# Statistics by channel tiles, a late bias and later last products in a fused attention block

## The chip, the cores and the metric

The kernel runs on one core of a Trainium2 chip. The metric is the device time of one execution in microseconds (us). The time before is 2275.32 us, the median of three runs (2275.29 to 2275.84). A core has a matrix engine (TensorE, PE in the profile), a vector engine (VectorE, DVE), an activation engine (ScalarE, ACT), a general engine (GpSimd, POOL), and queues that start transfers (DMA); SyncE (SP) issues most of these here. The engines run side by side and wait for each other by semaphores. PSUM is the memory that TensorE writes its products to, SBUF the memory for everything else.

## The reference

x has 384 channels of 192 x 192 pixels. Layer 0 normalises x by groups of 12 channels, makes q, k and v by a 1 x 1 product, takes the maximum of each 2 x 2 block, applies a 3 x 3 filter per channel, and mixes channels within 8 heads by four top-k softmaxes of the q-k products over all pixels. Layer 1 normalises again, takes signs, shifts rows and multiplies by signs of weights. Cut to what matters:

```python
def _gn(v, G=32, eps=1e-5):
    B_, C_, H_, W_ = v.shape
    g = v.reshape(B_, G, C_ // G, H_, W_)
    m = jnp.mean(g, axis=(2, 3, 4), keepdims=True)
    s = jnp.var(g, axis=(2, 3, 4), keepdims=True)
    return ((g - m) / jnp.sqrt(s + eps)).reshape(v.shape)

def _L0_conv_ref(x, w_qkv, b_qkv, w_dw, b_dw, w_proj, b_proj, temperature, a1, a2, a3, a4):
    # ...
    qkv = jnp.einsum('bchw,oc->bohw', x, w_qkv) + b_qkv[None, :, None, None]
    qkv = qkv.reshape(b, 3 * c, hs, DS, ws, DS).max(axis=(3, 5))
    qkv = lax.conv_general_dilated(qkv, w_dw, (1, 1), 'SAME', feature_group_count=3 * c, ...)
    q, k, v = jnp.split(qkv + b_dw[None, :, None, None], 3, axis=1)
    # ... reshaped to (b, HEADS, C, hw), q and k divided by their norms
    attn = jnp.einsum('bhcn,bhdn->bhcd', q, k) * temperature[None]
    out = _topk_softmax(attn, C // 2) @ v * a1 + _topk_softmax(attn, C * 2 // 3) @ v * a2 \
        + _topk_softmax(attn, C * 3 // 4) @ v * a3 + _topk_softmax(attn, C * 4 // 5) @ v * a4
    out = jax.nn.gelu(out.reshape(b, c, hs, ws), approximate=False)
    out = jnp.repeat(jnp.repeat(out, DS, axis=2), DS, axis=3)
    return jnp.einsum('bchw,oc->bohw', out, w_proj) + b_proj[None, :, None, None]

x = x + _L0_conv_ref(_gn(x), ...)
x = x + _L1_conv_ref(_gn(x), ...)   # signs, a shift of rows, a product with signs of weights
```

## The kernel before

x is cut into 24 units of 8 rows (2304 KB each; 128 partitions x 3 channel tiles x 1536 pixels). The pool `big` has 8 buffers of that size. The program goes through x three times: once for the statistics, once for q, k and then v, once for the end. A scheduler orders the instructions of each engine by priority (mostly the order of the program) unless the program pins them.

In the first pass, whole units go in turn to ScalarE (every third) and VectorE:

```python
        stats = [p1.tile([P, CT, BATCH * (UPX // 512) * 6], F32, name=f"stats{i}") for i in range(NB)]
        mv = p1.tile([P, CT, NB, 2], F32, name="mv")
        acc = p1.tile([P, CT, 2, NU // SHARE], F32, name="acc")
        wg = p1.tile([NG, 3 * C], F32, name="wg")
        seen = 0
        for i in range(NU):
        for i in range(NU):
            u = NU - 1 - i
            xt = unit(u, parts=CT if u in (0, NU - 1) else 1)
            # ... cut: the last six units are kept; small, indT and wq are loaded at i == 0
            if i % SHARE == 0:
                for t in range(CT):
                    for k, f in enumerate((AF.Identity, AF.Square)):
                        junk = p1.tile([P, UPX], BF16, name="junk")
                        nc.scalar.activation(
                            junk, xt[:, t], f, accum_out=acc[:, t, k, i // SHARE : i // SHARE + 1]
                        )
            else:
                b, k = divmod(seen, BATCH)
                seen += 1
                for t in range(CT):
                    for j in range(UPX // 512):
                        at = (k * (UPX // 512) + j) * 6
                        nc.vector.bn_stats(stats[b][:, t, at : at + 6], xt[:, t, j * 512 : (j + 1) * 512])
                    if k == BATCH - 1:
                        nc.vector.bn_aggr(mv[:, t, b, :], stats[b][:, t, :])
            # ... cut: at u == NU // 2, wg = sums of the weights by group
        sums = p1.tile([P, CT, 2], F32, name="sums")
        more = p1.tile([P, CT, 2], F32, name="more")
        nc.vector.tensor_reduce(more, acc, AX.X, ALU.add)
        sq = p1.tile([P, CT, NB], F32, name="sq0")
        nc.vector.tensor_mul(sq, mv[:, :, :, 0], mv[:, :, :, 0])
        nc.vector.tensor_add(sq, sq, mv[:, :, :, 1])
        nc.vector.tensor_reduce(sums[:, :, 0], mv[:, :, :, 0], AX.X, ALU.add)
        nc.vector.tensor_reduce(sums[:, :, 1], sq, AX.X, ALU.add)
        nc.vector.scalar_tensor_tensor(sums, more, 1.0 / (BATCH * UPX), sums, ALU.mult, ALU.add)
        ps = psp.tile([NG, 2], F32, name="gsps")
        group_sums(ps, sums)

        gs = p1.tile([NG, 2], F32, name="gs")
        nc.vector.tensor_scalar_mul(gs, ps, BATCH / (NU * GRP))
        gv = p1.tile([NG, 2], F32, name="gv")
        nc.vector.tensor_scalar_mul(gv[:, 0:1], gs[:, 0:1], -1.0)
        var = p1.tile([NG, 1], F32, name="var")
        nc.vector.scalar_tensor_tensor(var, gs[:, 0:1], gv[:, 0:1], gs[:, 1:2], ALU.mult, ALU.add)
        nc.vector.tensor_scalar_add(var, var, 1e-5)
        inv_sqrt(p1, gv[:, 1:2], var, 1, "s0", NG)
        ps = psp.tile([P, CT, 2], F32, name="spread")
        spread(ps, gv)
        nc.vector.tensor_copy(rstd0, ps[:, :, 1])

        for c0, c1 in ((0, P), (P, 2 * C), (2 * C, 3 * C)):
            for t in range(CT):
                nc.vector.tensor_scalar_mul(wq[:, t, c0:c1], wq[:, t, c0:c1], rstd0[:, t : t + 1])
        nc.vector.tensor_copy(nmean0, ps[:, :, 0])
        shift = p1.tile([NG, 1], F32, name="shift")
        nc.vector.tensor_mul(shift, gv[:, 0:1], gv[:, 1:2])
        ps = psp.tile([P, NM], F32, name="bqps")
        for m in range(NM):
            nc.tensor.matmul(ps[:, m : m + 1], wg[:, m * P : (m + 1) * P], shift, start=True, stop=True)
        nc.vector.tensor_add(bq, bq, ps)
```

Then a unit's tile m (0 to 2 are q, 3 to 5 k, 6 to 8 v) is made in three blocks of three products, each reduced from PSUM by VectorE, followed by a bias on ScalarE and nine taps of the filter (the first on ScalarE, eight on VectorE):

```python
    def qkv_unit(pqkv, xt, u, m, pl, parts):


        x4 = xt.rearrange("p t (r w) -> p t r w", w=W)
        lo, hi = rows(u)
        for r0, nr, c0, ncol in BLOCKS:
            ps = pqkv.tile([P, 512], F32, name="qkv")
            for t in range(CT):
                nc.tensor.matmul(
                    ps,
                    wq[:, t, m * P : (m + 1) * P],
                    x4[:, t, r0 : r0 + nr, c0 : c0 + ncol],
                    start=(t == 0),
                    stop=(t == CT - 1),
                )
            nc.vector.tensor_reduce(
                pl[:, 2 + r0 // 2 : 2 + (r0 + nr) // 2, 1 + c0 // 2 : 1 + (c0 + ncol) // 2],
                ps.rearrange("p (i a j b) -> p i j a b", a=2, b=2, j=ncol // 2),
                AX.XY,
                ALU.max,
            )
        new = pl[:, 2 : 2 + PR, 1 : 1 + WP]
        nc.scalar.activation(new, new, AF.Identity, bias=bq[:, m : m + 1])
        for acc, r0, n in parts:
            acc2 = acc.rearrange("p (r w) -> p r w", w=WP)
            for k in range(9):
                r = lo - 1 + r0 + k // 3
                src = pl[:, r : r + n, k % 3 : k % 3 + WP]
                if k == 0:
                    nc.scalar.activation(acc2, src, AF.Identity, bias=bdw[:, m : m + 1], scale=wdw[:, m, 0:1])
                else:
                    nc.vector.scalar_tensor_tensor(acc2, src, wdw[:, m, k : k + 1], acc2, ALU.mult, ALU.add)
            # ... cut: ScalarE keeps two rows for the next unit
    pqkv = products_of_x.enter_context(tc.tile_pool(name="qkv", bufs=3, space=PSUM))
```

q and k are transposed in blocks by VectorE, moved by 32 transfers into `room`, and multiplied into `gram` one unit later; the last unit's products come in `gathered`, at the start of v:

```python
        size = -(-(PR + 1) * WP // P) * C
        blocks = wp.tile([P, 2, size], F32, name="blocks")
        nc.gpsimd.memset(blocks, 0.0)
        pool = padded(wp, 2 * CT)
        room = big.tile([P, CT, UPX], F32, name="room", tag="big").rearrange("p t n -> p (t n)")
        qkT = room[:, : 2 * size].rearrange("p (s n) -> p s n", s=2)
        # ... cut
        def products(u):

            n, nk, q, k = of_unit(u)
            for i in range(nk):
                L = min(P, n * WP - i * P)
                for t in range(CT):
                    nc.tensor.matmul(
                        gram[t][:, : BN[t] * B],
                        q[:L, t, i],
                        k[:L, B0[t] : B0[t] + BN[t], i],
                        start=u == 0 and i == 0,
                        stop=u == NU - 1 and i == nk - 1,
                    )
        # ... cut
            for m in range(2 * CT):
                acc = tp.tile([P, (PR + 1) * WP], F32, name="dw")[:, : n * WP]
                qkv_unit(pqkv, xt, u, m, pool[m], [(acc, 0, n)])
                transposed(u, *divmod(m, CT), acc)
                sq = tp.tile([P, (PR + 1) * WP], BF16, name="sq", bufs=1)
                nc.scalar.activation(sq[:, : n * WP], acc, AF.Square, accum_out=ssq[:, m, u : u + 1])
                if u and m == CT - 1:
                    products(u - 1)
                if m % CT == CT - 1:
                    moved(u, m // CT)

    def gathered():

        products(NU - 1)
        for t in range(CT):
            at = D0[t] - B0[t] * B
            nc.vector.tensor_copy(gsb[:, t, : DN[t]], gram[t][:, at : at + DN[t]])
        last_products.close()
```

In v's loop, the softmax is a generator that is advanced once for each tile from the second unit on, and the attention products follow when it is done:

```python
        wl = wp.tile([P, CT, C], F32, name="wl")
        nc.scalar.dma_start(wl, a["w_projG"].rearrange("(t p) o -> p t o", p=P))
        nc.vector.tensor_reduce(wg1, wl.rearrange("p t (g c) -> p t g c", c=GRP), AX.X, ALU.add)
        wl = wp.tile([P, CT, C], F32, name="wl")
        nc.scalar.dma_start(wl, a["weightT"].rearrange("(t p) o -> p t o", p=P))
        nc.scalar.activation(wb, wl, AF.Sign, saturate=False)
        done, steps = 0, None
        # ... cut
        for u in range(NU):
            # ... cut: the unit's load, chunk (the output of v), parts
            for m in range(CT):
                # ... cut
                qkv_unit(pqkv, xt, u, 2 * CT + m, pool[m], parts)
                if u == 0 and m == 1:
                    gathered()
                    po = vs.enter_context(tc.tile_pool(name="p4o", bufs=NP, space=PSUM))
                    psp = vs.enter_context(tc.tile_pool(name="p3ps", bufs=1, space=PSUM))
                    bg = psp.tile([P, P], F32, name="p3ps")[:NG, :1]
                    group_sums(bg, bpr.unsqueeze(2))
                    nc.vector.tensor_scalar_mul(bg1, bg, -1.0 / GRP)
                if u >= TOPK and steps is None:
                    steps = softmaxes(p3, psp)
                if steps:
                    if next(steps, 1):
                        steps = ()
                        scratch.close()
                        early = opened("p5x0", 1)
                elif steps == () and done < NAB - HOLD and (done + 1) * ABLK <= first * WP:
                    attention(done)
                    done += 1
```

## Time and profile before

| | |
|---|---|
| time, median of three runs | 2275.32 us |
| span of the profiled execution | 2274.4 us |
| PE busy | 2093.8 us (92%) |
| DVE busy | 1902.4 us (84%) |
| ACT busy | 819.4 us (36%) |
| products of q, k and v (L321) | 1683.9 us in 3888 entries, 594 ns mean |
| filter taps on DVE (L344) | 709.1 us (q and k), 370.2 us (v) |
| reductions from PSUM (L328) | 442.6 us in 648, 684 ns mean |
| statistics on DVE (L248) | 87.2 us in 144, 675 ns mean |
| statistics on ACT (L239) | 71.1 us in 48, 1482 ns mean |

A product of 32-bit numbers shows as two entries on PE (x18 for 9 products). Entries overlap with the next, so a mean duration is longer than the time from one start to the next; where the pace matters, starts are compared. In the profile, an idle time stands in brackets with what ended it, and a name such as `room<-blocks` is a transfer or an operation from the right tile to the left one. L and a number is a line of the kernel.

The stages, by the profile's time: loads and statistics to about 152 us, a chain of small operations to 161 us, q and k to about 1345 us, v to about 1970 us, the end to 2274 us.

### The profile page before, as it was taken

What the parts mean: (1) busy time and instruction counts of PE and PEld (TensorE: products, weight loads), DVE (VectorE), ACT (ScalarE), POOL (GpSimd) and SP (SyncE); (2) the same over time, 40 slices, a digit from 0 to 9 for tenths busy, and PEclk for the clock granted to TensorE, in tenths of its full rate; (3) what the DMA queues carried; (4) which work ended last, traced back from release to release, by engine and by line L of the source; (5) the groups of instructions that cost most, each with busy time, mean ns of one, the idle gap of its engine ahead of it and who ended that gap; (6) DMA issues with size and microseconds to landing.
All of it is one profiled execution on the core that took longest, in us unless ns stands there. A gap on an engine that the chain in (4) does not pass through costs nothing.

```text
span 2274.4 us, 19469 instructions
## 1 busy us (share of the span) xinstructions
PE 2093.8 (92%) x6135; PEld 995.7 (44%) x6135; DVE 1902.4 (84%) x3269; ACT 819.4 (36%) x1418; POOL 211.3 (9%) x338
## 2 busy tenths in 40 slices
PE   1029999999999999999999979999999999999998
PEld 0014444444444444444444434443444444455554
DVE  4667888888888888888888878987787888889998
ACT  4532222222222222222222212225333233397885
POOL 0000000000000000000000000000000000087775
PEclk7559999999999999999999989999999999999999
DMA  9962222232222232222222212105221212279997
GB/s 397 417 267 59 67 63 69 67 101 69 70 63 68 68 90 80 71 63 66 70 79 89 71 40 94 42 0 208 84 83 42 93 74 84 83 282 392 425 425 307
DMA packets 208727, 300.30 MB, mean 132 GB/s; under 512 B 162000, under 2 KB 164848, under 8 KB 208624
## 3 DMA queue, kind: packets, MB, share of 16 engines
q1 hardware_dynamic: 197936, 243.46, 30.8%
q10 hardware_dynamic: 10688, 55.61, 6.0%
q8 instruction: 48, 0.79, 0.1%
q14 instruction: 55, 0.45, 0.1%
HBM read 213.68 MB, written 56.62 MB: 119 GB/s over the span
## 4 chain that ended last, share of the span: by engine, by line
PE 79%; DVE 11%; DMA 6%; ACT 2%; issue 1%; SPq 1%; ACTq 0%; POOL 0%; POOLq 0%; DVEq 0%
PE qkv L321 64%; PE l1ps L743 6%; DMA xt<-in_x_dram 5%; PE yps L559 5%; DVE chunk L344 5%; PE gram L412 3%; DVE pooled L328 2%; PE ops L594 2%; DVE dw L344 1%; DVE stats L248 1%; ACT signs L724 1%; ACT chunk L342 0%; ACT pooled L335 0%; SPq L401 0%; DVE xt L751 0%
## 5 line engine op out<-in xcount | busy, mean ns | idle before, releaser
L321 PE MATMUL qkv<-xt,wq 128*128 128x512 f32 x3888 | 1683.9, 594 | 0.3 <-DVE small L294 0.3
L321 PEld LDWEIGHTS qkv<-xt,wq 128*128 128x128 f32 x3888 | 738.3, 191 | 920.3 <-issue 824.2
L344 DVE SCALAR_TENSOR_TENSOR dw<-pooled,small,dw 128x384 f32<-128x384 f32 (+2 forms) x1152 | 709.1, 616 | 118.8 <-ACT dw L342 93.7
L328 DVE TENSOR_REDUCE pooled<-qkv 128x128 f32<-128x512 f32 x648 | 442.6, 684 | 73.5 <-PE qkv L321 73.0
L344 DVE SCALAR_TENSOR_TENSOR chunk<-pooled,small,chunk 128x384 f32<-128x384 f32 (+3 forms) x696 | 370.2, 546 | 74.7 <-ACT chunk L342 57.3
L346 ACT COPY pooled<-pooled 128x196 f32<-128x196 f32 x207 | 73.6, 356 | 764.4 <-DVE dw L344 543.0
L335 ACT ACTIVATE pooled<-pooled,small 128x384 f32<-128x384 f32 x216 | 133.0, 616 | 409.4 <-DVE pooled L328 401.9
L724 ACT ACTIVATE signs<-xt,nmean 64x1536 fp8e4<-64x1536 f32 x144 | 226.5, 1573 | 49.0 <-PE yps L559 23.6
L743 PE MATMUL l1ps<-signs,wb 128*128 128x384 fp8e4 x864 | 154.5, 329 | 6.3 <-POOL signs L716 4.8
L751 DVE SCALAR_TENSOR_TENSOR xt<-l1ps,small,xt 128x768 f32<-128x768 f32 x144 | 138.9, 1009 | 6.3 <-ACT signs L724 3.6
L559 PE MATMUL yps<-chunk,wpr 128*128 128x384 f32 x396 | 138.3, 487 | 0.4 <-DVE xt L568 0.4
L568 DVE SCALAR_TENSOR_TENSOR xt<-yps,small,xt 128x768 f32<-128x768 f32 x132 | 128.0, 1012 | 12.2 <-DMA xt<-in_x_dram 4.7
L248 DVE BATCH_NORM_STATS2 stats<-xt 128x6 f32<-128x512 f32 x144 | 87.2, 675 | 60.4 <-DMA xt<-in_x_dram 60.4
L743 PEld LDWEIGHTS <-wb 128*128 128x128 fp8e4 x864 | 84.1, 97 | 80.4 <-issue 20.9
L198 PE MATMUL gsps<-sums,small 128*32 128x2 f32 x6 | 0.5, 196 | 128.2 <-DVE sums L269 128.2
L433 ACT ACTIVATE sq<-dw 128x384 bf16<-128x384 f32 (+2 forms) x144 | 75.3, 523 | 117.0 <-DVE dw L344 117.0
L302 POOL MEMSET pooled<- 128x196 f32 x9 | 2.4, 265 | 1173.2 <-DVE dw L344 1155.8
L342 ACT ACTIVATE dw<-pooled,small 128x384 f32<-128x384 f32 (+2 forms) x144 | 100.4, 698 | 2.3
L559 PEld LDWEIGHTS yps<-chunk,wpr 128*128 128x128 f32 x396 | 73.3, 190 | 41.4 <-PE yps L559 1.6
L239 ACT ACTIVATE junk<-xt 128x1536 bf16<-128x1536 f32 x48 | 71.1, 1482 | 52.1 <-DMA xt<-in_x_dram 50.9
L383 DVE STREAM_TRANSPOSE blocks<-dw 128x384 f32<-128x384 f32 (+1 forms) x144 | 82.0, 570 | 3.4
L412 PE MATMUL gram<-room 128*128 128x160 f32 (+3 forms) x438 | 68.1, 310 | 15.5 <-DMA room<-blocks 15.5
(117 smaller groups left out, 639.6 us busy)
## 6 DMA issues: line engine op xcount, KB each, us to landing
xt<-in_x_dram SPq DMA_DIRECT2D x83, 2304.0 KB, 14.0
out_dram<-xt ACTq DMA_DIRECT2D x19, 2304.0 KB, 15.4
room<-blocks SPq DMA_DIRECT2D x736, 36.0 KB, 2.0
xt<-in_x_dram SPq DMA_DIRECT2D x18, 768.0 KB, 8.9
out_dram<-xt ACTq DMA_DIRECT2D x9, 768.0 KB, 7.9
out_dram<-xt SPq DMA_DIRECT2D x6, 768.0 KB, 6.6
wq<-in_w_qkvT_dram ACTq DMA_DIRECT2D x1, 1728.0 KB, 15.7
room<-blocks SPq DMA_DIRECT2D x32, 48.0 KB, 2.1
```

The source lines that it names most:

```text
L248: nc.vector.bn_stats(stats[b][:, t, at : at + 6], xt[:, t, j * 512 : (j + 1) * 512])
L321: nc.tensor.matmul(ps, wq[:, t, m * P : (m + 1) * P], x4[:, t, r0 : r0 + nr, c0 : c0 + ncol], start=(t == 0), stop=(t == CT - 1),)
L328: nc.vector.tensor_reduce(pl[:, 2 + r0 // 2 : 2 + (r0 + nr) // 2, 1 + c0 // 2 : 1 + (c0 + ncol) // 2], ps.rearrange("p (i a j b) -> p i j ...
L335: nc.scalar.activation(new, new, AF.Identity, bias=bq[:, m : m + 1])
L342: nc.scalar.activation(acc2, src, AF.Identity, bias=bdw[:, m : m + 1], scale=wdw[:, m, 0:1])
L344: nc.vector.scalar_tensor_tensor(acc2, src, wdw[:, m, k : k + 1], acc2, ALU.mult, ALU.add)
L412: nc.tensor.matmul(gram[t][:, : BN[t] * B], q[:L, t, i], k[:L, B0[t] : B0[t] + BN[t], i], start=u == 0 and i == 0, stop=u == NU - 1 and i ...
L559: nc.tensor.matmul(ps, wpr[:, t, m * P : (m + 1) * P], o[:, t, :], start=(t == 0), stop=(t == CT - 1),)
L568: nc.vector.scalar_tensor_tensor(x5[:, m, r], yb, bpr[:, m : m + 1], x5[:, m, r], ALU.add, ALU.add)
L724: nc.scalar.activation(rows_of(sg, p, SAT[t] - HSHIFT[t][h]), xt[p, t, :].rearrange("p (r w) -> p r w", w=W), AF.Sign, bias=nmean1[p, t : ...
L743: nc.tensor.matmul(ps[:, j, : 2 * W], wb[:, t, m * P : (m + 1) * P], rows_of(sg, slice(0, P), SAT[t])[:, r0 + 2 * j : r0 + 2 * j + 2], sta ...
L751: nc.vector.scalar_tensor_tensor(blk, ps[:, :, : 2 * W], bl1[:, m : m + 1], blk, ALU.add, ALU.add)
```

## The change

It has five parts. (1) Statistics: of every unit, one channel tile goes to ScalarE and two to VectorE, with results in one tile `part` that both write; scale factors are folded into ScalarE's operations and the eps into a constant column. The scratch for it lies in `room`, which is now allocated ahead of the first pass, and the last two units arrive in three parts. (2) The zeros of `blocks` and of the padded tiles of q and k are written ahead of the first pass. (3) The bias from the group means is computed inside the first tile of q, after its products, instead of before it. (4) The last products of q and k and what follows are pinned to program order behind v's third tile instead of its second. (5) Softmax operations are pinned in program order, and the loads of w_projG and weightT with their reduction and sign move from the start of v to its units 4 and 5. The aim is less time in which TensorE stands: at the start, and where q and k pass over to v.

The diff, cut (statements that only move with the part around them are left out):

```diff
+    wg = aT.rearrange("p t c -> p (t c)")[:NG]
+    shift = ap.tile([NG, 1], F32, name="shift")
@@ ahead of the first pass
+    pairs = ctx.enter_context(ExitStack())
+    wp = right("p2w", stack=pairs)
+    size = -(-(PR + 1) * WP // P) * C
+    blocks = wp.tile([P, 2, size], F32, name="blocks")
+    nc.gpsimd.memset(blocks, 0.0)
+    padded_qk = padded(wp, 2 * CT)
+    room = big.tile([P, CT, UPX], F32, name="room", tag="big").rearrange("p t n -> p (t n)")
@@ the first pass
+        size1 = CT * BATCH * (UPX // 512) * 6
+        stats = [room[:, i * size1 : (i + 1) * size1].rearrange("p (t n) -> p t n", t=CT) for i in range(NB)]
+        junk = room[:, NB * size1 : NB * size1 + UPX // 2].bitcast(BF16)
+        part = p1.tile([P, CT, 2, NB + NU // SHARE + 1], F32, name="part")
+        measure = 1.0 / (BATCH * UPX)
+        nc.vector.memset(part[:, :, 0, NB + NU // SHARE :], 0.0)
+        nc.vector.memset(part[:, :, 1, NB + NU // SHARE :], 1e-5 * NU / BATCH)
-            xt = unit(u, parts=CT if u in (0, NU - 1) else 1)
+            xt = unit(u, parts=CT if u in (0, 1, NU - 1) else 1)
-            if i % SHARE == 0:
-                # all three tiles on ScalarE
-            else:
-                # all three tiles on VectorE
+            for t in range(CT):
+                if t == u % SHARE:
+                    at = NB + i // SHARE
+                    for k, f, scale in ((0, AF.Identity, measure), (1, AF.Square, measure**0.5)):
+                        nc.scalar.activation(junk, xt[:, t], f, scale=scale, accum_out=part[:, t, k, at : at + 1])
+                    continue
+                b, k = divmod(seen[t], BATCH)
+                seen[t] += 1
+                for j in range(UPX // 512):
+                    at = (k * (UPX // 512) + j) * 6
+                    nc.vector.bn_stats(stats[b][:, t, at : at + 6], xt[:, t, j * 512 : (j + 1) * 512])
+                if k == BATCH - 1:
+                    nc.vector.bn_aggr(part[:, t, :, b], stats[b][:, t, :])
@@ the chain after it
-        nc.vector.tensor_reduce(more, acc, AX.X, ALU.add)
-        # ... two reductions and a scaled sum more
-        nc.vector.tensor_scalar_mul(gv[:, 0:1], gs[:, 0:1], -1.0)
-        nc.vector.tensor_scalar_add(var, var, 1e-5)
-        ps = psp.tile([P, NM], F32, name="bqps")
-        for m in range(NM):
-            nc.tensor.matmul(ps[:, m : m + 1], wg[:, m * P : (m + 1) * P], shift, start=True, stop=True)
-        nc.vector.tensor_add(bq, bq, ps)
+        nc.vector.tensor_mul(sq, part[:, :, 0, :NB], part[:, :, 0, :NB])
+        nc.vector.tensor_add(part[:, :, 1, :NB], part[:, :, 1, :NB], sq)
+        nc.vector.tensor_reduce(sums, part, AX.X, ALU.add)
+        nc.vector.tensor_scalar_mul(gv[:, 0:1], ps[:, 0:1], -BATCH / (NU * GRP))
+    def bias(ps):
+        for m in range(NM):
+            nc.tensor.matmul(ps[:, m : m + 1], wg[:, m * P : (m + 1) * P], shift, start=True, stop=True)
+        nc.vector.tensor_add(bq, bq, ps)
@@ qkv_unit, after the three blocks
+        if before:
+            before(pqkv.tile([P, 512], F32, name="qkv")[:, :NM])
@@ products
-                    nc.tensor.matmul(
+                    ins = nc.tensor.matmul(
+                    if u == NU - 1:
+                        tc.keep_in_program_order(ins)
@@ q and k
-                qkv_unit(pqkv, xt, u, m, pool[m], [(acc, 0, n)])
+                qkv_unit(pqkv, xt, u, m, padded_qk[m], [(acc, 0, n)], None if u or m else bias)
@@ softmax
-        nc.vector.tensor_reduce(ss, ssq, AX.X, ALU.add)
+        tc.keep_in_program_order(nc.vector.tensor_reduce(ss, ssq, AX.X, ALU.add))
-                    nc.vector.memset(some, TAKEN)
+                    tc.keep_in_program_order(nc.vector.memset(some, TAKEN))
@@ v
-        # wl <- w_projG and its reduction to wg1, wl <- weightT and its sign to wb, ahead of v's loop
+        def weights(name):
+            wl = wp.tile([P, CT, C], F32, name="wl")
+            tc.keep_in_program_order(nc.scalar.dma_start(wl, a[name].rearrange("(t p) o -> p t o", p=P)))
+            return wl
+                if m == 0 and u == UC:
+                    wl = weights("w_projG").rearrange("p t (g c) -> p t g c", c=GRP)
+                    tc.keep_in_program_order(nc.vector.tensor_reduce(wg1, wl, AX.X, ALU.add))
+                if m == 0 and u == UC + 1:
+                    tc.keep_in_program_order(nc.scalar.activation(wb, weights("weightT"), AF.Sign, saturate=False))
-                if u == 0 and m == 1:
+                if u == 0 and m == CT - 1:
                     gathered()
```

## The prediction

> **What bounds the kernel now.** I read the windows table first: it says which engine limits each stage. Columns: window and length in us, then busy us (instructions) of PE, PEld, DVE, ACT and POOL, PE clock, DMA share, GB/s.
>
> ```profile
> 61.00:101.00 40.00, 0.00 (x0) 0.00 (x0) 28.33 (x48) 19.28 (x25) 0.00 (x0) 0.50 1.02 418
> 140.00:152.00 12.00, 0.00 (x0) 0.00 (x0) 11.89 (x22) 5.34 (x7) 0.00 (x0) 0.50 0.85 351
> 152.00:161.00 9.00, 5.84 (x31) 5.67 (x31) 5.71 (x28) 0.20 (x1) 0.22 (x1) 0.50 0.00 0
> 235.00:1267.00 1032.00, 1032.00 (x2665) 488.96 (x2664) 900.11 (x1520) 273.71 (x634) 0.00 (x0) 1.00 0.26 73
> 1340.00:1377.00 37.00, 21.46 (x67) 11.44 (x66) 21.57 (x48) 5.62 (x12) 1.54 (x6) 0.77 0.19 54
> 1377.00:1450.00 73.00, 73.00 (x176) 32.67 (x175) 67.00 (x199) 16.74 (x29) 0.00 (x0) 1.00 0.26 97
> 1450.00:1485.00 35.00, 35.00 (x82) 15.42 (x82) 34.96 (x101) 7.76 (x15) 0.00 (x0) 1.00 0.00 1
> 1552.00:1970.00 418.00, 417.93 (x1243) 178.72 (x1243) 331.02 (x614) 144.60 (x335) 2.20 (x2) 1.00 0.23 86
> ```
>
> Until 140 us the load of x is the limit (DMA share 1.0, 418 GB/s). From 161 us to about 1970 TensorE is, except in two places: 140 to 161 us, where statistics and their tail run alone, and 1340 to 1377, where PE is busy 21 of 37 us. From there to 1485 VectorE has almost no slack beside a full PE. The chain of waits names DVE lines there, but PE does not stop, so PE's own record decides.
>
> The chain of waits at the first place (start, length):
>
> ```profile
> 140.11 7.81 DVE stats L248 x13
> ...
> 155.38 1.44 PE spread L203 x6
> 156.82 3.85 PE bqps L293 x18
> ...
> 160.91 19.51 PE qkv L321 x38
> ```
>
> DVE works off two whole units (18 statistics, 0.60 us apart) after the last load it waits for; then a chain of small steps, then 18 bias entries on PE before the first product. The timelines of PE, DVE and ACT at the second place, with the idle time before an entry in brackets:
>
> ```profile
> 1344.47 0.35 PE L198 MATMUL p3ps<-small 128*32 128x1 f32 x6
> 1360.37 0.87 PE L412 MATMUL gram<-room 128*128 128x160 f32 x2 [15.54 <-DMA room<-blocks]
> 1361.03 9.83 PE L321 MATMUL qkv<-xt,wq 128*128 128x512 f32 x18
> 1393.59 135.78 PE L321 MATMUL qkv<-xt,wq 128*128 128x512 f32 x316
> ```
>
> ```profile
> 1347.15 1.85 DVE L328 TENSOR_REDUCE pooled<-qkv 128x128 f32<-128x512 f32 x3
> 1360.35 0.30 DVE L455 TENSOR_REDUCE ss<-ssq 128x6 f32<-128x144 f32 x1 [11.35 <-DMA room<-blocks]
> ```
>
> ```profile
> 1364.20 0.38 ACTq L582 DMA_DIRECT2D wl<-in_weightT_dram  x1
> 1368.06 1.16 ACT L583 ACTIVATE wb<-wl 128x1152 fp8e4<-128x1152 f32 x1 [3.02 <-DMA wl<-in_weightT_dram]
> ```
>
> PE stands 15.5 us because the first of the last q and k products comes right after v's first tile, and its operand is still being moved. The row with 316 entries runs at 135.78/316 = 0.430 us each, the same as in q and k: v is at PE's rate. A tile of v (18 entries) is 7.73 us.
>
> **What the skill says.** (1) The Trainium skill, TensorE: Matmul & The Clock Gate, "What's actually happening": the array runs at half clock after an idle window of about 3.4 us and needs about as long of work to recover. The trace agrees: after the stall 18 entries take 9.83 us instead of 7.73, and the first product phase starts with 26 entries in 14.36 us instead of 11.2. (2) The Trainium skill, DMA: Bandwidth & Descriptors, "Where 436 GB/s comes from": the port ceiling is 435 GB/s. The trace shows 418, so I expect nothing from the load. (3) The Trainium skill, Perfetto Trace Analysis, "Identifying the Most-Contended Engine": matmul busy time is a poor measure of the roofline, VectorE's a fair one. So I take PE's pace, not its 92%, and 34.96 of 35 us on DVE at its word.
>
> **The change, part by part.**
>
> *Statistics by channel tile.* Before, a unit was all DVE (9 x 0.60 = 5.44 us) or all ACT (6 x 1.61 = 9.7 us). Now each gives two tiles to DVE (3.6 us) and one to ACT (3.2 us), both under the 5.65 us between landings (DVE starts on loads at 106.2, 123.2, 128.8, 140.1). Nothing queues. Unit 1 lands by 140.1, so unit 0's last third lands at about 145.75 (estimate: one spacing later). Unit 0's first tile is ACT's; DVE's last three statistics and one aggregate (0.4) end at 148.0 instead of 152.07: 4.05 us saved. One buffer less for x (room is taken early) still leaves about six loads in flight.
>
> *Shorter chain.* From the last aggregate, five overlapped steps (0.82 us) become three (about 0.65); the eps step (0.18) and one dependency (0.08) go: 0.4 us.
>
> *Late bias.* Before, the first product started 4.09 us after the spread ended, behind the bias. Now it waits only for a copy and the first scaled weights, about 0.55 us (the scaling began 0.19 us after the copy): 3.55 us earlier. The 18 bias entries move behind tile 0's 18 products. Those last about 11 us, so PE is at full clock and they cost half of 3.85, about 1.95 us (estimate). Net 1.6 us.
>
> *Zeros ahead.* The blocks memset (2.66 us from 160.78) and the pads ended at 165.6, before the first reduction at 166.44. With products starting near 153 they would be late; moved, they cost nothing.
>
> Start of the kernel: 4.05 + 0.4 + 1.6 = about 6.0 us. Q and k then run at PE's pace, and the order of instructions there is the same.
>
> *Last products behind v's third tile.* PE removes 15.54 us of idle time, 0.35 us of the small product (now at the start), and the cold clock: from 1360.37 to 1374.07, 13.70 us for 18 product entries (7.73) and 24 gram entries (3.48 at 0.145), so 2.5 us. Against that, tile two of v needs a PSUM buffer of tile one. There are three, and DVE gets to the first reduction only at 1347.15 (0.6 us): PE waits about 3.2 us, just short of an idle window. After that DVE, which stood 11.35 us, does tile one's taps while PE does tiles two and three (15.5 us, to about 1363, on the old clock); the moved operand is there at 1360.3. No other wait. Net 15.54 + 0.35 + 2.5 - 3.2 = 15.2 us.
>
> *Softmax and weights later.* The softmax steps (about 20.5 us of DVE in start-to-start spacing, another 1.26 for the reduction of w_projG) now all fall from v's fourth tile on, two or three us of them that used to sit in the stall. I walked through the changed DVE order with these costs: reduction 0.60, tap 0.53 if another operation stands between, 0.655 if not, small operations at their spacing. From tile 6 to tile 18 DVE needs about 94 us against PE's 93, having fallen about 2.5 us behind at the first softmax step. PE can run 5.2 us ahead (two blocks of 2.58). One place breaks that: in u = 4, ACT issues the load of w_projG after its copy of tile 0's rows, some 1.9 us of DVE work before DVE's reduction of it. Issue to use took 3.86 us for the like load (1364.20 to 1368.06), plus 0.4 for the copy, so DVE stands about 2.4 us where it has no slack. Lag about 6.3 against 5.2: PE loses about 1.1 us. I add 0.5 for small misses. From tile 18 on DVE recovers; the order from the transposes on is as before.
>
> Middle: 15.2 - 1.6 = 13.6 us. The sum is 19.6 us: 2275.3 - 19.6 = **2255.7 us**.
>
> **Rivals.** (A) *VectorE takes over in v.* Its 34.96 of 35 us speaks for it; removing PE's stall would only move it to DVE. If DVE fell behind steadily, up to 8 us of the 15 would come back as PE waits on reductions: 2264. Against it: 11 us of DVE idle time are freed at the same place, and tiles after the softmax need only 6.0 to 7.0 of 7.73 us. (B) *The front gain is only half.* If the last load lands later, or the bias is no cheaper in line, 2 to 3 us are lost: 2258. For it: the order of landing of thirds is not seen in the old trace, since DVE was behind. (C) *The gap of 3.2 us still cools the clock*: 2.5 us back, 2258. (D) *All goes well*, no wait on w_projG: 2254. (E) *The end takes it back*: the last 264 us have DMA share 0.95, but all their loads depend on buffers that v frees, so they shift with it; I give that little.
>
> **Range and chances.** Most misses cost 1 to 8 us, few gain more than 3. I say 2251 to 2264. Faster by 2% needs 2230, 26 us less than my estimate, and more than all idle time touched here; slower by 2% needs a failure that nothing in the order shows. Faster 0.01, same 0.98, slower 0.01.
>
> **What would show it.** First product at about 153 us (160.9 before), bias entries about 0.1 us each; DVE's last statistic at about 147.6. No gram wait on room; one PE wait of about 3 us before v's second tile; entries there at 0.43, not 0.86. A DVE wait on wl of about 2.4 us in u = 4 and a PE wait of about 1 us behind it. The prediction is wrong if PE shows many waits on DVE reductions between v's fourth and eighteenth tile, if loads run below 415 GB/s, or if the stage after v is longer than before.

## The result and the profile after

The changed kernel takes 2256.79 us (median of four runs, 2255.86 to 2259.91) against 2275.58 us before: a ratio of 0.9919 with a 95% interval of 0.9901 to 0.9936. That is 18.8 us less, within 2%; the prediction said 2255.7.

First the windows table of the changed kernel, with the columns of before (window and length in us; busy us of PE, PEld, DVE, ACT and POOL; PE clock; DMA share; GB/s):

```profile
61.00:101.00 40.00, 0.00 (x0) 0.00 (x0) 27.16 (x46) 22.42 (x29) 0.00 (x0) 0.50 1.01 417
140.00:152.00 12.00, 0.98 (x9) 0.89 (x9) 8.60 (x24) 6.11 (x8) 0.00 (x0) 0.50 0.85 351
152.00:161.00 9.00, 8.22 (x15) 3.95 (x15) 3.94 (x12) 0.00 (x0) 0.00 (x0) 0.57 0.00 0
1335.00:1364.00 29.00, 25.70 (x72) 12.91 (x72) 21.94 (x41) 5.97 (x13) 1.66 (x6) 0.94 0.11 28
1437.00:1472.00 35.00, 35.00 (x83) 15.58 (x82) 34.90 (x102) 7.87 (x15) 0.00 (x0) 1.00 0.05 18
```

The load of x is as it was (417 GB/s). From 140 to 152 us DVE is no longer full (8.60 of 12), and from 152 to 161 us PE already works 8.22 of 9 us. The place between k and v, where PE was busy 21 of 37 us, is now 25.70 of 29. In v, DVE is as full as before (34.90 of 35) and PE still has 35.00.

The chain of waits at the first place:

```profile
143.88 1.89 DVE room L276 x3
145.77 0.02 issue
145.80 0.48 DVE part L278
146.28 1.74 DVE room L276 x3
148.02 0.02 issue
148.04 0.49 DVE part L278
```

DVE now follows the landing of the last unit's thirds and has two sets of three statistics left, not thirteen. Between the two stands an aggregate of 0.48 us that the prediction had left out. The timelines of PE at both places, then of DVE and of ACT's queue (idle time before an entry in brackets, and what ended it):

```profile
151.50 1.43 PE L203 MATMUL spread<-gv,indT 32*128 32x2 f32 x6 [1.69 <-DVE gv L193]
153.71 11.00 PE L331 MATMUL qkv<-xt,wq 128*128 128x512 f32 x18 [0.78 <-DVE wq L309]
164.64 2.16 PE L316 MATMUL qkv<-shift,aT 32*128 32x1 f32 x18
...
1343.01 17.41 PE L331 MATMUL qkv<-xt,wq 128*128 128x512 f32 x36 [3.30 <-DVE pooled L338]
1360.26 3.64 PE L415 MATMUL gram<-room 128*128 128x160 f32 x24
```

```profile
1342.14 0.23 DVE L389 STREAM_TRANSPOSE blocks<-dw 128x96 f32<-128x96 f32 x1
1342.30 1.85 DVE L338 TENSOR_REDUCE pooled<-qkv 128x128 f32<-128x512 f32 x3
...
1451.49 1.34 DVE L631 TENSOR_REDUCE wg<-wl 128x96 f32<-128x1152 f32 x1
```

```profile
1447.04 0.37 ACTq L586 DMA_DIRECT2D wl<-in_w_projG_dram  x1
```

The wait on room before gram is gone: 24 gram entries follow the 36 of v's second and third tile at once. In its place stands the wait that the prediction named, 3.30 us for a PSUM buffer: DVE comes to v's first reduction at 1342.30, when it has transposed the last tile of k. But the 36 entries take 17.41 us; at the 7.73 us per tile of before they would take 15.46. So half clock behind the pause costs 1.9 us. And the reduction of w_projG at 1451.49 has no bracket: DVE did not wait for that load, which was issued 4.45 us earlier.

Three marks divide both executions: the first gram product of unit 22 (the last but one of q and k), the first product with the projection weights (the end of v), and the end. Times in us, from the profiled executions:

| kernel | start to mark 1 | mark 1 to end of v | end of v to the end |
|---|---|---|---|
| before | 1313.45 | 656.53 | 304.4 |
| changed | 1308.61 | 642.98 | 303.0 |
| difference | 4.84 | 13.55 | 1.4 |
| predicted | 6.0 | 13.6 | 0 |

The profiled pair differs by 19.8 us, the medians by 18.8.

### The profile page after: what moved, and what is told of

Same layout as the page of the kernel before. It is cut to its first block, busy times and chain, and to the rows that moved or that the text cites. A ratio compares the mean times of both kernels' runs of the same rounds, so it can differ in the third digit from the quotient of the medians.

```text
span 2254.6 us, 19480 instructions
## 1 busy us (share of the span) xinstructions
PE 2090.4 (93%) x6135; PEld 991.7 (44%) x6135; DVE 1902.2 (84%) x3267; ACT 819.7 (36%) x1418; POOL 211.3 (9%) x338
## 4 chain that ended last, share of the span: by engine, by line
PE 79%; DVE 11%; DMA 6%; ACT 2%; issue 1%; ACTq 0%; POOL 0%; SPq 0%; POOLq 0%; DVEq 0%
PE qkv L331 64%; DMA xt<-in_x_dram 6%; PE l1ps L752 5%; PE yps L564 5%; DVE chunk L356 5%; PE gram L415 3%; DVE pooled L338 2%; PE ops L597 2%; DVE dw L356 1%; ACT signs L733 1%; DVE xt L760 1%; ACT chunk L354 0%; ACT pooled L347 0%; DVE xt L573 0%; DMA small<-in_small_dram 0%
## 5 line engine op out<-in xcount | busy, mean ns | idle before, releaser
L276 DVE BATCH_NORM_STATS2 room<-xt 128x6 f32<-128x512 f32 x144 | 88.1, 676 | 49.1 <-DMA xt<-in_x_dram 49.1
L270 ACT ACTIVATE room<-xt 128x1536 bf16<-128x1536 f32 x48 | 71.2, 1483 | 55.8 <-DMA xt<-in_x_dram 55.0
L711 POOL COPY rest<-signs 9x384 int32<-9x384 int32 (+1 forms) x144 | 72.3, 502 | 70.6 <-ACT signs L733 65.1
## 6 DMA issues: line engine op xcount, KB each, us to landing
wq<-in_w_qkvT_dram ACTq DMA_DIRECT2D x1, 1728.0 KB, 15.1
```

## The experiments

The theory from these two traces: the parts add; the start is worth a little less than predicted; in the middle a pause of 3.3 us and the half clock behind it remain, and both go if PE has another PSUM buffer. Rivals: VectorE is the real limit in v; the late bias is what the start gained from; the end gained because the rest came earlier. The same three marks of all twelve kernels stand in the table at the end of this section. The zeros written ahead and the pins on the softmax had no run of their own.

### The start alone, the middle alone

`start_only` is the changed kernel with the middle of before:

```diff
-                    if u == NU - 1:
-                        tc.keep_in_program_order(ins)
-                if u == 0 and m == CT - 1:
+                if u == 0 and m == 1:
                     gathered()
```

and with both weight loads ahead of v's loop and no pins on the softmax. `middle_only` is the kernel before with these lines the other way round.

> Only the start is changed (statistics by channel tile, shorter chain, zeros ahead, late bias); the last q and k products, the softmax and the weight loads stand as before. Theory 'the parts add, and the start is worth what the pair of traces shows at the end of q and k': first product at 153.7 us, the last product of unit 22 about 4.8 us earlier than before, a stall of about 15.5 us on room in v as before, end of v about 4.8 us earlier, time about 2270.5 us. My prediction's own sum says 6.0 us: 2269.3. Rival 'the start is swallowed by the transition': DVE or the transfers, not PE, set the time at which the stall ends, so the stall grows by what the start gives, and the time stays near 2275. Rival 'the end gained 1.4 us because everything comes earlier': the stage after v is about 1.4 us shorter here too, 2269.

> Only the middle is changed (last q and k products pinned behind v's third tile, softmax steps and weight loads later); the start is as before. Theory 'the parts add': first product at 160.9 us as before; in v one PE wait of about 3.3 us before the second tile and half clock for about 36 entries after it (17.4 us in place of 15.5); v ends about 13.1 to 13.5 us earlier than before; time about 2262, or 2260.7 if the end stage's 1.4 us belong to this part. No DVE wait on the first of the two weight loads. Rival 'as predicted, 13.6 with a DVE wait of 2.4 us on w_projG': the load is issued under 2.5 us before its reduction.

Measured: 2270.48 us (ratio 0.9976, 0.9967 to 0.9985) and 2262.30 us (0.9941, 0.9926 to 0.9956): 5.2 and 13.4 us less than 2275.68. They sum to 18.6; both together gave 18.8. The parts add. PE's timeline of the start alone, and of the middle alone:

```profile
1354.56 0.87 PE L415 MATMUL gram<-room 128*128 128x160 f32 x2 [15.35 <-DMA room<-blocks]
```

```profile
1346.60 15.69 PE L321 MATMUL qkv<-xt,wq 128*128 128x512 f32 x36 [3.13 <-DVE pooled L328]
```

The stall on room shifts with the start and keeps its length, so it isn't set by something absolute. Most of it is the time in which SyncE starts the sixteen transfers of the last three tiles of k (SP's timeline of the kernel before; 10.24 us in the start alone):

```profile
1347.10 10.26 SPq L401 DMA_DIRECT2D room<-blocks  x16
```

Starting them from two queues, which attacks the stall itself, was not tried. The line of the middle alone is a surprise: a pause of 3.13 us, and then 36 entries at full clock. The clock behind such a pause is a matter of luck, and for that reason the theory's 13.1 to 13.5 us are too few in this execution (15.1 between the marks); the median of the times agrees with them.

### The bias ahead of the products

```diff
-    def bias(ps):
-        for m in range(NM):
+        ps = psp.tile([P, NM], F32, name="bqps")
+        for m in range(NM):
             nc.tensor.matmul(ps[:, m : m + 1], wg[:, m * P : (m + 1) * P], shift, start=True, stop=True)
```

> The changed kernel with the bias computed ahead of the first product, as before the change. Theory 'out of the way it saves what it costs cold minus what it costs in line': the first product starts about 3.5 us later than 153.7 (the 18 entries take 3.85 us and wait for the scaled weights' successors on DVE), the 2.10 us in line go, so q and k are about 1.4 to 1.6 us later at the last product of unit 22; time about 2258.3. Rival 'the entries ahead also warm the clock': the products after them reach full clock earlier by the same span, the difference at unit 22 is under 0.5 us.

Measured: 2257.87 us (2257.57 to 2258.42). PE's timeline:

```profile
152.60 3.97 PE L314 MATMUL bqps<-shift,aT 32*128 32x1 f32 x18
156.83 18.52 PE L329 MATMUL qkv<-xt,wq 128*128 128x512 f32 x38 [0.26 <-DVE small L315]
...
1342.88 18.54 PE L329 MATMUL qkv<-xt,wq 128*128 128x512 f32 x36 [3.13 <-DVE pooled L336]
```

The first product is 3.1 us later than in the changed kernel, 2.1 us of bias entries in line are gone, and mark 1 is at 1308.38. The nine kernels with the late bias and no fill products at the start have it at 1307.2 to 1308.9, 1308.1 on average: the late bias is worth about 0.3 us, within their scatter. That is the number of the rival (under 0.5 us). Its reason, that the entries ahead also warm the clock, is not shown. Behind them 38 entries take 18.52 us, 2.2 more than at full rate (38 x 0.43), and behind the late start of the changed kernel 18 entries take 11.00, 3.3 more than 7.73. But the other eight kernels with the late bias lose 1.9 to 3.3 us there. The two with the old start, where the bias is ahead as well, lose 3.1 (before: 61 entries in 29.38 us) and 1.6 (`middle_only`: 64 in 29.15). Of the 1.4 us between the two profiled executions, 1.1 are the half clock at the second place: 18.54 us for the 36 entries in place of 17.41.

### One or two more PSUM buffers

```diff
+    pqx = last_products.enter_context(tc.tile_pool(name="qkx", bufs=1, space=PSUM))
+    turn = [pqkv, pqkv, pqkv, pqx]
 # in qkv_unit; from gathered() on, turn is [pqkv] again
-            ps = pqkv.tile([P, 512], F32, name="qkv")
+            turn.append(turn.pop(0))
+            ps = turn[-1].tile([P, 512], F32, name="qkv")
```

This is `banks1`; `banks2` differs by

```diff
-    pqx = last_products.enter_context(tc.tile_pool(name="qkx", bufs=1, space=PSUM))
-    turn = [pqkv, pqkv, pqkv, pqx]
+    pqx = last_products.enter_context(tc.tile_pool(name="qkx", bufs=2, space=PSUM))
+    turn = [pqkv, pqkv, pqkv, pqx, pqx]
```

> The changed kernel with two more PSUM buffers for the products of x until gram is collected (five in place of three). Theory 'the 3.3 us before v's second tile is a wait for a PSUM buffer, and it is this gap that cools the clock': the gap vanishes (five blocks are 12.9 us of products, DVE comes to its first reduction about 3 us after v's first tile is done), the 36 entries after it take 15.5 us instead of 17.4, VectorE has the slack to take it (it is idle about 5 us of the 73 before the softmax steps), and the time falls by about 5 us to 2251.8. Rival 'VectorE is the bound there': the gap only moves; PE waits on DVE reductions later in v, between its third and its twelfth tile, and the gain is 1 to 2 us (the clock) or none. In this version the scheduler also puts the small bias product behind the last q and k products again, about 0.35 us of PE.

> The changed kernel with one more PSUM buffer for the products of x until gram is collected (four in place of three); otherwise the order is the changed kernel's, with the small bias product at the very start. Theory 'a pause's length counts[...]': one block is 2.58 us, so the wait of 3.1 to 3.3 us before v's second tile shrinks to 0.5 to 0.7 us, too short to be followed by half clock; the 36 entries after it take 15.5 to 15.7 us; time within 1 us of the version with two more buffers (2252.9). Rival 'two are needed': a wait of over 2 us stays, because DVE comes later to its first reduction, and the time lies at 2254 or above.

Measured: 2252.89 us with two (2252.71 to 2253.27), **2251.93 us with one** (2251.19 to 2252.85; ratio to before 0.9895, 0.9880 to 0.9909). PE's timeline with one:

```profile
1341.62 13.14 PE L332 MATMUL qkv<-xt,wq 128*128 128x512 f32 x30 [0.73 <-DVE pooled L339]
1354.60 3.64 PE L418 MATMUL gram<-room 128*128 128x160 f32 x24
```

The pause shrinks by one block, from 3.30 to 0.73 us, the 30 entries after it run at 0.438 us, and mark 1 to end of v is 4.2 us shorter (638.74). With two buffers there is no pause at all and 0.5 us more are gained there (638.26), too little to see in the time. VectorE has the slack: later in v no PE waits appear but those of the changed kernel. This version beats both kernels.

### Filling the pauses at the start

`start_warm` is `banks1` plus

```diff
+        warm = psp.tile([P, 512], F32, name="warm", bufs=1)
+        for _ in range(6):
+            nc.tensor.matmul(warm, wq[:, 0, :P], kept[1][:, CT - 1, :512], start=True, stop=True)
         sums = p1.tile([P, CT, 2], F32, name="sums")
```

`start_warm2` has three more and holds this tail, down to `shift`, in program order. The results of these products are not used.

```diff
+        with tc.manual_schedule():
             # the six products, then the tail of the statistics, indented
             group_sums(ps, sums)
+            warmed(2)
             # ...
             spread(ps, gv)
+            warmed(1)
```

> As the version with one more PSUM buffer, and in addition six products of 128x512 whose result is not used, from about 140 us (they read the last third of unit 1), ahead of the small group products. Theory 'the first products are slow because TensorE has stood still, and nothing else': with the clock already full the first 18 products take 7.73 to 8.2 us in place of 10.2 to 11.0, the 18 bias entries stay near 2.1 us, and q and k are 2 to 3 us earlier at the last product of unit 22 (1305 to 1306); time 2 to 3 us less. Rival 'they are slow because their operands are': the first products wait for DVE's scaling of the weights one by one, then 18 products stay near 10 us and the time is unchanged. Rival 'the pause of 1.7 us between the small products cools it again': 18 products stay above 9 us.

> As the version with one more PSUM buffer, with nine products of 128x512 whose result is not used: six from about 140 us as in the run before, two in the pause of 1.7 us behind the small group products, one between the spread and the first product of q; the tail of the statistics is kept in program order. Theory 'the pauses of 0.8, 1.7 and 0.8 us around the small products let the clock fall back in the run before': with them filled the first 18 products take 7.73 to 8.2 us, q and k are about 2 us earlier at the last product of unit 22 than with one more buffer alone (1307.2), that is 1305 to 1305.5, and the time is 2249.5 to 2251 if the end stage draws the same. Rival 'the fill products get in the way': spread or the first product start later by up to 1 us, and the gain is under 1 us. Rival 'the operands are what is slow': 18 products stay at 9.6 us.

Measured: 2253.22 us (2252.95 to 2253.75) and 2258.65 us (2255.24 to 2258.68, of which the profiled execution is the shortest). PE's timeline of each:

```profile
140.28 8.36 PE L292 MATMUL warm<-xt,wq 128*128 128x512 f32 x12 [115.96 <-DMA xt<-in_x_dram]
149.47 0.35 PE L198 MATMUL gsps<-sums,small 128*32 128x2 f32 x6 [0.84 <-DVE sums L299]
151.51 0.82 PE L203 MATMUL spread<-gv,indT 32*128 32x2 f32 x6 [1.69 <-DVE gv L193]
153.12 9.63 PE L339 MATMUL qkv<-xt,wq 128*128 128x512 f32 x18 [0.78 <-DVE wq L316]
```

```profile
152.48 1.13 PE L292 MATMUL warm<-xt,wq 128*128 128x512 f32 x2
157.02 9.39 PE L342 MATMUL qkv<-xt,wq 128*128 128x512 f32 x18 [3.42 <-DVE shift L321]
```

In the first the clock was full at the spread (0.82 us in place of 1.43), and the 18 entries still took 9.63: three pauses of 0.84, 1.69 and 0.78 us with little work between them came before half clock. That is the last rival of its expectation. Slow operands are not the cause: PE waits nowhere within the 18 entries, and the granted clock in the four microseconds from 153 us is 0.53, 0.50, 0.50 and 0.77, then 1.00. It won 0.6 us at mark 1 and nothing in time, since its end stage is 2.5 us longer. The second missed its purpose: the fill product reads the weights that DVE scales, so DVE waited for it (0.90 us), and program order put the first product behind `shift`: a pause of 3.42 us. Whether a fill that reads something else would bring the 2 us was not tried.

### The weight loads early, gram one tile sooner, no pin, unit 1 whole

Four short edits of the changed kernel, one for each run in this order (`weights_early` takes the loads' lines out of v's loop as well, with their pins):

```diff
+        wl = wp.tile([P, CT, C], F32, name="wl")
+        nc.scalar.dma_start(wl, a["w_projG"].rearrange("(t p) o -> p t o", p=P))
+        nc.vector.tensor_reduce(wg1, wl.rearrange("p t (g c) -> p t g c", c=GRP), AX.X, ALU.add)
+        # ... the same for weightT and its signs, then v's loop
```

```diff
-                if u == 0 and m == CT - 1:
+                if u == 0 and m == 1:
                     gathered()
```

```diff
-                    if u == NU - 1:
-                        tc.keep_in_program_order(ins)
```

```diff
-            xt = unit(u, parts=CT if u in (0, 1, NU - 1) else 1)
+            xt = unit(u, parts=CT if u in (0, NU - 1) else 1)
```

> The changed kernel with the loads of w_projG and weightT, the reduction and the signs made of them ahead of v's loop, as before the change; the last products of q and k stay behind v's third tile. Theory 'their place matters little': DVE's reduction (1.26 us) and ScalarE's wait for the second load (about 3 us) fall into v's first tiles, where DVE is what TensorE waits for, so the wait before v's second tile grows from 3.3 to 4 to 8 us, and with it the chance of half clock; DVE then has 1.26 us less to do between v's fourth and eighteenth tile; 1 to 5 us more in all: 2258 to 2262. Rival 'the loads take the place of the moved blocks on the DMA engines': the last q and k products wait for room too. Rival 'no effect': ScalarE is ahead and absorbs it, 2256.8.

> The changed kernel with the pinned last products of q and k behind v's second tile in place of the third. Theory 'the moved blocks are in room at about 1354.5 us (there the stall ended in the version with the start alone)': v's second tile ends at 1351 to 1353, TensorE waits 2 to 4 us on room, with or without half clock behind it; time 2 to 6 us more than the changed kernel: 2259 to 2263. Rival 'transfers are faster when nothing else is asked of the queues': no wait on room, and the same time.

> The changed kernel without the pin on the last products of q and k; they stand in the program behind v's third tile, but the scheduler takes the first of them ahead, to behind v's first tile. Theory 'it is the pin, not the place in the program, that removes the stall': TensorE waits about 15.4 us on room behind v's first tile, less what the wait before the second tile would have been, and the time goes up by about 12 us to 2268 to 2270. Rival 'the later weight loads removed the stall': no wait above 4 us, the time as in the changed kernel.

> The changed kernel with the last but one unit of the first pass loaded whole, as before, in place of in three parts. Theory 'DVE's tail is set by the last unit alone': unit 1 is there at about 140.1 us, its two tiles on DVE take 3.6 us, to 143.7, just before the last unit's first third for DVE is there (143.9): first product within 0.5 us of 153.7, time the same within 1 us. Rival 'the parts also bring the last unit forward, or spread the work on DVE': last statistics 1 to 2 us later and the first product with them.

Measured: 2265.76 us (2264.59 to 2266.88), 2257.62 us (2256.42 to 2258.74), 2268.76 us (one run), 2257.03 us (2256.15 to 2258.51). First ACT's timeline with the early loads, then PE's of it:

```profile
1348.90 0.38 ACTq L583 DMA_DIRECT2D wl<-in_w_projG_dram  x1
1349.33 0.61 ACT L347 ACTIVATE pooled<-pooled,small 128x384 f32<-128x384 f32 x1 [7.44 <-DMA room<-blocks]
```

```profile
1342.50 9.69 PE L331 MATMUL qkv<-xt,wq 128*128 128x512 f32 x18 [3.31 <-DVE pooled L338]
1356.79 9.65 PE L331 MATMUL qkv<-xt,wq 128*128 128x512 f32 x18 [4.60 <-DVE pooled L338]
```

Last DVE's line for the reduction of that load:

```profile
1353.80 1.35 DVE L584 TENSOR_REDUCE wg<-wl 128x96 f32<-128x1152 f32 x1 [2.60 <-DMA wl<-in_w_projG_dram]
```

ACT stands 7.44 us around the issue of the load, and what ends it is the blocks being moved to room: by the program's pools the load's buffer lies where the blocks were. Behind it in ACT's order is the bias of v's first tile, so DVE stands 7.04 us for ACT and 2.60 for the load itself. PE then stands 4.60 us before v's third tile, and half clock follows once more (9.65 us for 18 entries): 7.4 us more from mark 1 to the end of v, and 9.0 in time, where 1 to 5 were expected. The end stage is 3.6 us longer as well: PE waits 3.16 us for GpSimd's signs there, not 1.59, then does 10 products in 3.18 us, not 1.80, and waits 0.91 us for DVE, not 0.28. So the later loads are no cost of the change but a condition of it: with gram at the old place the same wait (7.51 us on ACT in the kernel before, 7.43 in the start alone) lay beside PE's own stall.

PE's timeline with gram one tile sooner, then without the pin:

```profile
1353.11 3.71 PE L415 MATMUL gram<-room 128*128 128x160 f32 x24 [1.23 <-DMA room<-blocks]
```

```profile
1354.17 0.87 PE L415 MATMUL gram<-room 128*128 128x160 f32 x2 [14.21 <-DMA room<-blocks]
```

One tile sooner, gram waits 1.23 us on room, less than the 2 to 4 expected. The second tile ends at 1351.9, inside the range expected, after half clock (9.69 us, as with the early loads); but room is there at 1353.1, not 1354.5. After mark 1 the moved blocks need 45.3 us in both kernels of this pair, 46.4 in the start alone and 46.9 before, where the load of w_projG runs beside them: that fits the rival, for 1.1 to 1.6 us. The time can't be told from the changed kernel's. Without the pin the stall is back: the pin does it, not the place in the program. Unit 1 in thirds is worth nothing.

### The pause in the end stage

`end_warm` is `banks1` with 12 products whose results are not used, behind the first unit's products of layer 1:

```diff
                     finished(i, m)
+                if i == 0:
+                    warm = psp.tile([P, 2, 512], F32, name="l1ps")
+                    for _ in range(12):
+                        nc.tensor.matmul(
+                            warm[:, 0, : 2 * W], wb[:, 0, :P],
+                            rows_of(signs[0], slice(0, P), SAT[0])[:, :2], start=True, stop=True,
+                        )
```

> As the version with one more PSUM buffer, and in addition 12 products of 128x384 whose result is not used, behind the first unit's products of layer 1, in the pause in which TensorE waits for the signs that GpSimd moves. Theory 'what the end stage gained in the changed kernel (263.4 us from the second group of products to the end, against 264.8 before) is the clock: 34 products took 5.74 us there, 7.40 before, because the pause was not followed by half clock in that one execution': with the pause filled they take 5.74 us every time, and the end from that group on takes about 263.5 us; against the version with one more buffer 0 to 1.7 us, by what that one draws. Rival 'the loads of the end set its length': the 34 products are faster, but the end stage stays between 264.5 and 265.5 us.

Measured: 2252.62 us (2251.18 to 2252.68), the same as without. PE's timeline of it:

```profile
1986.00 5.74 PE L756 MATMUL l1ps<-signs,wb 128*128 128x384 fp8e4 x34 [1.55 <-POOL signs L729]
...
1995.59 1.80 PE L756 MATMUL l1ps<-signs,wb 128*128 128x384 fp8e4 x10 [1.59 <-POOL signs L729]
```

The 34 products run at full clock, and then PE waits 1.59 us for the next signs. The clock is worth nothing there, where GpSimd sets the pace, and the theory for the end's 1.4 us falls. What does differ is a wait on loads about 60 us later. DVE's timeline of before and changed:

```profile
2069.41 1.94 DVE L568 SCALAR_TENSOR_TENSOR xt<-yps,small,xt 128x768 f32<-128x768 f32 x2 [2.55 <-DMA xt<-in_x_dram]
```

```profile
2049.72 1.94 DVE L573 SCALAR_TENSOR_TENSOR xt<-yps,small,xt 128x768 f32<-128x768 f32 x2 [2.32 <-DMA xt<-in_x_dram]
```

PE then waits for DVE 1.26 us before and 0.28 in the changed kernel: 1.0 of the 1.4 us. In `start_warm` DVE has three such waits (2.06, 2.70 and 2.06 us), and PE waits 0.38, 1.41 and 1.38. Counted from the 34 products on and without these waits of PE, the rest takes 263.1 to 263.7 us in eleven of the fourteen kernels, with 5.74 or 7.40 us for the 34 products alike. The other three are `banks2`, where they take 8.37, and the two with the wait of 3.16 or 3.17 us for signs (`weights_early`, `gram_second`). Why the loads land later in some executions stays open.

The stages are of the profiled execution, the time is the median:

| kernel | start to mark 1 | mark 1 to end of v | end stage | time |
|---|---|---|---|---|
| start_only | 1308.12 | 656.70 | 304.3 | 2270.48 |
| middle_only | 1312.10 | 641.42 | 305.3 | 2262.30 |
| bias_ahead | 1308.38 | 644.26 | 303.4 | 2257.87 |
| banks2 | 1307.83 | 638.26 | 305.0 | 2252.89 |
| banks1 | 1307.22 | 638.74 | 303.7 | 2251.93 |
| start_warm | 1306.64 | 638.74 | 306.2 | 2253.22 |
| start_warm2 | 1310.31 | 638.68 | 304.5 | 2258.65 |
| end_warm | 1307.66 | 638.71 | 304.4 | 2252.62 |
| weights_early | 1308.10 | 650.35 | 306.7 | 2265.76 |
| gram_second | 1307.79 | 644.45 | 304.7 | 2257.62 |
| unpinned_gram | 1308.86 | 654.14 | 304.0 | 2268.76 |
| unit1_whole | 1308.40 | 642.97 | 304.4 | 2257.03 |

## Why the prediction was right, and where its terms were off

- **Statistics and chain: right, a little too large.** The last aggregate ends at 148.53, not 148.0: the term left out the aggregate of the last but one tile (0.48 us). Statistics and chain without the late bias bring the first product from 160.91 to 156.83, 4.1 us, where the terms sum to 4.45.
- **Late bias: mis-sized.** Said 1.6 us, gave about 0.3. Said 3.55 us earlier less 1.95 in line; measured 3.3 (from the spread's end to the first product 4.10 us with the bias ahead, 0.78 without) less 2.10, which is 1.2. The rest goes into half clock behind the first product, which the term took to be the same: it costs 3.3 us in the changed kernel, 2.2 with the bias ahead. That part is not clear of the scatter (1.9 to 3.3 with the late start). The start as a whole gave 4.84 in this pair.
- **Zeros ahead cost nothing: as far as seen.** No wait on them shows at the first reductions; DVE waits for PE there (2.99 us).
- **Last products behind v's third tile: right in kind.** No wait on room; the pause for a PSUM buffer is 3.30 us (said 3.2). The failed step is "just short of an idle window": the clock did fall back, which cost 1.9 us (rival C). With the pause cut to 0.73 us by one more buffer it didn't.
- **The wait on w_projG: wrong.** The step took 1.9 us of DVE work between issue and use; in the trace DVE does most of one reduction, another one, nine taps and a softmax operation there, 4.45 us, more than the 3.8 us that the load needs to land. So the 1.1 us of PE and the 0.5 for misses are not there (rival D).
- **The middle's sum was right by two errors of opposite sign.** From the traces: stall 15.54 to 3.30 (12.24), small product 0.35, half clock 2.5 to 1.9 (0.6), one wait of the transposes less (0.61 and 0.91 us before, one of 0.88 now: 0.6), a new wait of 0.26 us at the softmax's first product: 13.5 us. The errors: half clock 1.9 us too much, the wait on w_projG 1.6 us that did not come. That the total came within 1.1 us of the median is luck in part: the start gave 1.2 us less than said, and the end 1.4 that were not foreseen.
- **Rival A (VectorE takes over): no.** With one and two more buffers PE came to the end of v 4.2 and 4.7 us sooner (from mark 1) without a new wait on DVE. **Rival B (half the front): in part**, 1.2 us of the 6.0. **Rival E: no**; the end stage moved with v and 1.0 of its 1.4 us are a shorter wait on a load.

## What to carry to other kernels

A stall on a transfer can be filled by work that is already there, if a pin holds it against the scheduler, and if everything else that waits for the same memory (here a weight load at the head of ScalarE's order) is moved too. Then look at what bounds the engine next: here three PSUM buffers, and a fourth, free until gram is collected, was worth a further 4.9 us. A pause of 2 to 3.5 us is to be priced as a range (here 0.2 to 3.1 us where PE set the pace), not as nothing.

## What the runs showed of the hardware

- Pauses of PE of 3.13 to 3.31 us were followed by anything from 0.2 us lost to half clock (`middle_only`: 36 entries in 15.69 us) over 1.9 (changed kernel, and the same 17.41 us in `unit1_whole`) to 3.1 (`bias_ahead`: 18.54 us). In the end stage, pauses of 2.19 and 2.20 us were followed by 34 products of 128x384 fp8e4 in 5.74 us once (changed kernel) and in 7.40 three times (`start_only`, `unit1_whole`, `unpinned_gram`). The Trainium skill, TensorE: Matmul & The Clock Gate, "What's actually happening", calls the window of about 3.4 us free-running; that agrees with a spread at the same pause. It also puts half clock behind at least one idle window; here shorter pauses were enough, and the measurement decides. Pauses of 0.73 and 0.74 us cost nothing in four kernels.
- Several short pauses may add up: in one execution 0.84, 1.69 and 0.78 us within 4.5 us, with 1.2 us of small products between them, came before half clock, where the clock had been full.
- Behind the same start, the first 18 entries took 9.59 to 11.00 us in the nine kernels with the late bias. With the old start, before and `middle_only` differ by 1.35 us at mark 1 (1313.45 and 1312.10). So differences of about 1 us at mark 1 say little in a single profile.
- The sixteen transfers from blocks to room took SyncE 10.26 us to start (before; 10.24 to 10.26 in five other kernels), so 0.64 us each.
